# Decoder layer: the cross-attention units of a query tile handled in pairs, their value matmuls placed behind the self-attention values in four column groups of 32

## Chip, cores, metric

One NeuronCore of a Trainium2 chip runs the whole program. The metric is device time in microseconds (us) of one launch, lower is better.

## The reference

Thirty-two independent sequences ("batches") of 256 tokens and 256 features go through one decoder layer, in fp32. Each step adds its input and is followed by a layer norm without weights.

```python
x = layernorm(x + self_attention(x))       # 16 heads of 64, 4 key/value heads, rotary, ALiBi
x = layernorm(x + cross_attention(x, ctx)) # 16 heads of 16, layer norms with weights ahead of all four
                                           # projections; a query sees the keys of its window of 64 and
                                           # of the window before, causal, and only where cell ids agree
x = layernorm(x + feed_forward(x))         # silu(gate) * up -> down, 256 -> 1024 -> 256, weights rounded
                                           # to three values, activations to 8 bits
```

## The kernel before

Tokens are cut into two query tiles of 128 for each batch. Self-attention of a batch is eight units (`self_units`: tile, key/value pair, head pair), two to a **period**. A period is four **slots**, and the loop at the end of the kernel writes out by hand, slot by slot, the order of all work of TensorE (PE), VectorE (DVE) and ScalarE (ACT). A batch has four periods, and batch follows batch without a gap. The other parts of a layer are generators that start at a given slot (`at`) and give one piece of work whenever `parts()` is called: projections (`self_inputs`), `self_output`, `cross_inputs`, `cross_output`, `feed_forward`. So at any time PE serves the self-attention of one batch, the cross attention and feed-forward of the batch before, and the projections of the next. The queue of SyncE (SP) issues nearly all transfers, in the order of the program.

In one period the order of a self unit pair `2m`, `2m+1` is: scores (tile `s`, L393, four matmuls of two 64-row blocks for each unit), reductions on DVE (L409, adding the ALiBi bias and keeping the maximum), exponentials on ACT (L427), transposes on PE (tile `t`, L471), copies out on ACT (L480). In the first slot of the next period come the values (tile `o`, L492, two column blocks of 64), then a normalizing product on DVE (L505), which waits for reciprocals that travel through a DMA transpose (`wide`, `planes`) and a GpSimd copy (`R`). `self_output` (tile `wo`, L513) follows for each query tile.

Cross attention has four units for a batch, one to a period, four periods behind (`CROSS = 4`): a unit is one query tile `qc` and one half `ch` of the 16 heads. Its steps are

- `cross_scores` in slot 1: tile `xs` in four PSUM banks, L674, blocks of 32 rows of the array. Query tile 0 is one span of 128 queries; tile 1 is two spans of 64 queries, each with its own keys, so its blocks are 32 rows by 64 columns. Then eight reductions on DVE (L688, mask added), 128 x 128 each;
- `cross_exp` in slots 2 and 3, on ACT (L704);
- `cross_turn` in slot 0 of the next period: transposes (`xt`, L713) and a copy on ACT (`xpT`, L715);
- `cross_values` in slot 1 of that period: tile `xo`, L729, four column blocks of 32, copied out by ACT (`xoT`, L738);
- `cross_back` in slot 2: transposes (`xr`, L749), reciprocal and product on DVE (L754, L755) into `on`.

`cross_output` (tiles `zoT`, `xw`) and `feed_forward` (`ff` gate and up, L816; `ffo`, L863; tanh on ACT, L830; products on DVE, L831 and L837) follow. PSUM has eight banks in one pool, all tiles of 128 x 512 fp32 share them. Buffers in SBUF have a number of copies, the last argument of `work`.

The order of the slots before:

```python
if part == 0:   # scores and exponentials of the two self units, then
    pair(self_values, m - 1)
    cross(cross_turn, k - 1, 0); cross(cross_turn, k - 1, 1)
elif part == 1:
    parts(); cross(cross_scores, k); cross(cross_values, k - 1)
elif part == 2: # self transposes and copies, then
    cross(cross_exp, k, 0); cross(cross_back, k - 1)
else:           # self transposes and copies, then
    cross(cross_exp, k, 1)
```

Of the kernel before, what the change touches and what calls it, by code (L numbers as in the profile page):

```python
# [9 lines left out]
F32 = mybir.dt.float32  # L10
# [3 lines left out]
AF = mybir.ActivationFunctionType  # L14
# [3 lines left out]
P = 128  # L18
L = 256
NT = L // P  # L20
D = 256
# [30 lines left out]
def kernel(  # L52
# [50 lines left out]
    def work(name, shape, bufs=2, dtype=F32):  # L103
        return sb.tile(list(shape), dtype, tag=name, name=name, bufs=bufs)

    def small(name, n):
        return sb.tile([P, 8], F32, tag="small", name=name, bufs=48)[:, 0:n]
# [100 lines left out]
    def prepare_cross():  # L208
# [4 lines left out]
        for j, (w, dst) in enumerate(  # L213
# [13 lines left out]
            if j == 0:  # L227
                nc.sync.dma_start(wo_sb, Wo.rearrange("(c p) n -> p c n", p=P))
            if j in xbias:
                more = work("xp", [P, 512])  # L230
                row = more[:, 0:D]
                nc.sync.dma_start(row, rows[j].partition_broadcast(P))
                for dc in range(NDC):
                    nc.gpsimd.tensor_scalar(
                        more[:, D + dc * P : D + (dc + 1) * P],
                        ones,
                        vecs_sb[:, j, 1, dc : dc + 1],
                        None,
                        ALU.mult,
                    )  # L240
# [238 lines left out]
        for pT, pt in zip(s["pT", i], s.pop(("t", i))):  # L479
            nc.scalar.copy(pT, pt)  # L480

    def self_values(b, m):

        s = state[b]
        qc, kc, _rp = self_units[2 * m]
        pTs = [s.pop(("pT", 2 * m + rp)) for rp in range(2)]
        s["oT", qc, kc] = oT = work("oT", [P, NCH // 2, P], 3)
        po = bank("o")
        for kk in range(NT):
            for rp in range(2):  # L490
                for half in range(2):
                    nc.tensor.matmul(  # L492
                        po[half * HD : (half + 1) * HD, rp * L : (rp + 1) * L],
                        s["v"][:, kk, (2 * kc + half) * HD : (2 * kc + half + 1) * HD],
                        pTs[rp][half][:, kk * L : (kk + 1) * L],
                        start=(kk == 0 and rp == 0),
                        stop=(kk == NT - 1 and rp == 1),
                    )
        s["po", m] = po

# [6 lines left out]
    def self_output(b, qc):  # L507
# [24 lines left out]
        yield  # L532
        zq = work("row", [P, D], 4)

        s["x1", qc] = x1 = work("x1", [P, D], 3)

        def residual():
            nc.vector.tensor_scalar(zq, h, mv[:, 0:1], rs[:, 1:2], ALU.subtract, ALU.mult)
# [120 lines left out]

    cross_units = [(qc, ch) for qc in range(NT) for ch in range(NDC)]

    spans = {0: ((0, P, 0, 0),), 1: ((0, 64, 64, NT), (64, P, P, 1))}

    def cross_scores(b, i):
        s = state[b]
        qc, ch = cross_units[i]

        banks = [bank("xs") for _ in range(4)]  # L670
        for q0, q1, k0, _t in spans[qc]:
            for r in range(4):
                rows_ = slice(r * 32, (r + 1) * 32)
                nc.tensor.matmul(  # L674
                    banks[r][:, 0 : 2 * P].rearrange("p (h k) -> p h k", k=P)[q0:q1],
                    s["xqT", qc][rows_, ch, q0:q1],
                    kTz[rows_, ch, :, k0 : k0 + P],
                    start=True,
                    stop=True,
                    tile_position=(r * 32, q0),  # L680
                )
        s["xnm", i] = [small("xnm", 4) for half in range(2)]
        for half in range(2):
            s["xp", i, half] = p = work("xp", [P, 512])
            for j in range(XHH):
                cols = slice(j * P, (j + 1) * P)

                nc.vector.tensor_tensor_reduce(  # L688
                    p[:, cols],
                    banks[2 * half + j // 2][:, j % 2 * P : (j % 2 + 1) * P],  # L690
                    s["mask"][:, qc, :],
                    -1.0,
                    3.0e38,
                    ALU.add,
                    ALU.min,
                    s["xnm", i][half][:, j : j + 1],
                )

    def cross_exp(b, i, half):
        s = state[b]  # L700
        p = s["xp", i, half]
        for j in range(XHH):
            cols = slice(j * P, (j + 1) * P)
            nc.scalar.activation(  # L704
                p[:, cols], p[:, cols], AF.Exp, bias=s["xnm", i][half][:, j : j + 1], scale=-1.0
            )

    def cross_turn(b, i, half):
        s = state[b]
        p = s.pop(("xp", i, half))  # L710
        pt = bank("xt")
        for j in range(XHH):
            nc.tensor.transpose(pt[:, j * P : (j + 1) * P], p[:, j * P : (j + 1) * P], ident)  # L713
        s["xpT", i, half] = pT = work("xpT", [P, 512])
        nc.scalar.copy(pT, pt)  # L715

    def cross_values(b, i):


        s = state[b]  # L720
        qc, ch = cross_units[i]
        po = bank("xo")
        for half in range(2):
            pT = s.pop(("xpT", i, half))
            h0 = ch * 2 * XHH + half * XHH
            for q0, q1, _k, t in spans[qc]:
                for j in range(XHH):
                    e0 = (t * XH + h0 + j) * XE
                    nc.tensor.matmul(  # L729
                        po[j * 32 : (j + 1) * 32, half * P + q0 : half * P + q1],  # L730
                        s["xv"][:, e0 : e0 + 32],
                        pT[:, j * P + q0 : j * P + q1],
                        start=True,
                        stop=True,
                        tile_position=(0, j * 32),
                    )
        s["xoT", i] = oT = work("xoT", [P, 2 * P])
        nc.scalar.copy(oT, po[:, 0 : 2 * P])  # L738

    def cross_back(b, i):  # L740

        s = state[b]
        qc, ch = cross_units[i]
        oT = s.pop(("xoT", i))
        if ch == 0:
            s["on", qc] = work("on", [P, D])
        pt = bank("xr")
        for half in range(2):
            nc.tensor.transpose(  # L749
                pt[:, half * P : (half + 1) * P], oT[:, half * P : (half + 1) * P], ident  # L750
            )
        po = pt[:, 0 : 2 * P].rearrange("p (h e) -> p h e", e=32)
        rinv = small("xrinv", 2 * XHH)
        nc.vector.reciprocal(rinv, po[:, :, XHD])  # L754
        nc.vector.tensor_tensor(  # L755
            s["on", qc][:, ch * P : (ch + 1) * P].rearrange("p (h e) -> p h e", e=XHD),
            po[:, :, 0:XHD],
            rinv.unsqueeze(2).to_broadcast([P, 2 * XHH, XHD]),
            ALU.mult,
        )  # L760

# [121 lines left out]
    def at(slot, gen):  # L883
        starts.setdefault(slot, []).append(gen)
# [5 lines left out]
    for b in range(B):  # L890
        s0 = 16 * b
        if b:
            at(s0 - 15, self_inputs(b))
        at(s0 + 2, cross_inputs(b))
        for t in range(NT):
            at(s0 + 9 + 8 * t, self_output(b, t))
            at(s0 + 4 * CROSS + 11 + 8 * t, cross_output(b, t))
        at(s0 + 4 * CROSS + 26, feed_forward(b))

    with tc.manual_schedule(engines={mybir.EngineType.PE, mybir.EngineType.DVE, mybir.EngineType.Activation}):  # L900
        running = []
        slot = min(starts)
        while starts or running:
            m, part = divmod(slot, 4)
            k = m - CROSS
            for gen in starts.pop(slot, ()):
                running.append([slot, gen])

            def cross(f, unit, *more):
                if 0 <= unit < 4 * B:  # L910
                    f(*divmod(unit, 4), *more)

            def pair(f, unit):
                if 0 <= unit < 4 * B:
                    f(*divmod(unit, 4))

            def own(f, unit, *more):
                if 0 <= unit < 8 * B:
# [11 lines left out]
            if part == 0:  # L930
                own(self_scores, 2 * m)
                own(self_exp, 2 * m, 0)
                own(self_exp, 2 * m, 1)
                flush()
                own(self_scores, 2 * m + 1)
                own(self_exp, 2 * m + 1, 0)
                pair(self_values, m - 1)
                cross(cross_turn, k - 1, 0)
                cross(cross_turn, k - 1, 1)
                parts()  # L940
                own(self_exp, 2 * m + 1, 1)
                pair(self_normal, m - 1)
            elif part == 1:
                parts()
                cross(cross_scores, k)
                cross(cross_values, k - 1)
            elif part == 2:
                pair(self_inverse, m)
                parts()
                own(self_turn, 2 * m)  # L950
                own(self_copy, 2 * m)
                cross(cross_exp, k, 0)
                cross(cross_back, k - 1)
            else:
                own(self_turn, 2 * m + 1)
                parts()
                own(self_copy, 2 * m + 1)
                cross(cross_exp, k, 1)
                pair(self_spread, m)
            if part < 3:  # L960
                flush()
# [91 lines left out]
```

## Time and profile before

| | us |
|---|---|
| median of 3 runs (lowest, highest) | 2183.65 (2179.22, 2185.29) |
| profiled execution, its span | 2184.1 |
| PE matmul busy | 2096.9 |
| PE weight loads busy | 1606.7 |
| DVE busy | 1778.0 |
| ACT busy | 1600.0 |
| GpSimd busy | 1285.1 |

The profile is of one execution. It gives the span from the first to the last instruction and no other time of its own, so the span is taken as its time; it lies 0.5 us from the median of the runs. Ends of matmuls are modelled in it, starts are measured. A group is one line, tile and shape; "xcount" counts records, and a matmul of fp32 operands leaves two, a transpose or a bf16 matmul one.

### The profile page before, as it was taken

The page shows a single profiled execution, that of the slowest core. Times are in us where ns is not written, and L with a number is a line of the kernel's source. Part 1 is how long each engine was busy: PE and PEld are TensorE (multiplying, and loading weights), DVE is VectorE, ACT ScalarE, POOL GpSimd, SP SyncE. Part 2 cuts the span into 40 slices and gives each one's busy share as a digit, 9 for nine tenths or more (in the row PEclk, how much of TensorE's full clock was granted, in tenths as well). Part 3 has the DMA queues.
Part 4 walks back from the last instruction along what each step waited for, and adds up shares of the span by engine and source line. Part 5 has one row for each costly group of instructions (what it writes and reads, how often), then busy time and mean ns, then how long its engine had stood idle before and what let it go on. Part 6 is the DMA issues. An engine that isn't in the chain of part 4 may idle for free.

```text
span 2184.1 us, 54367 instructions
## 1 busy us (share of the span) xinstructions
PE 2096.9 (96%) x17316; PEld 1606.7 (74%) x17316; DVE 1778.0 (81%) x6949; ACT 1600.0 (73%) x4833; POOL 1285.1 (59%) x1977
## 2 busy tenths in 40 slices
PE   7899999999999999999999999999999999999983
PEld 5677777777777777777777777777777777777751
DVE  4777888888888888888888888888888888888765
ACT  2478778777778877777877777877777877777862
POOL 4555665566655656655656655656666566666542
PEclk9899999999999999999999999999999999999986
DMA  7432333333333334334334333333343333333211
GB/s 219 111 75 72 82 75 83 77 79 86 89 72 78 83 71 91 86 71 86 76 76 89 82 77 79 78 81 83 86 82 76 81 82 74 90 81 69 53 42 32
DMA packets 326589, 177.57 MB, mean 81 GB/s; under 512 B 242976, under 2 KB 296096, under 8 KB 326304
## 3 DMA queue, kind: packets, MB, share of 16 engines
q1 hardware_dynamic: 324608, 170.52, 34.6%
q8 instruction: 139, 2.28, 0.5%
q10 hardware_dynamic: 1696, 3.57, 0.5%
q14 instruction: 146, 1.20, 0.2%
HBM read 39.50 MB, written 8.39 MB: 22 GB/s over the span
## 4 chain that ended last, share of the span: by engine, by line
PE 74%; DVE 11%; ACT 5%; POOL 4%; DMA 4%; issue 1%; SPq 0%; ACTq 0%; POOLq 0%; DVEq 0%
PE wo L513 10%; PE o L492 8%; PE proj L330 8%; PE t L471 8%; PE s L393 8%; PE ff L816 5%; PE xt L713 4%; PE xo L729 3%; PE xq L550 3%; PE xs L674 3%; PE ffo L863 3%; PE xk L622 3%; DVE p L409 2%; PE xw L775 2%; PE v L362 2%; DVE xib L805 2%
## 5 line engine op out<-in xcount | busy, mean ns | idle before, releaser
L427 ACT ACTIVATE p<-p,nm 128x256 f32<-128x256 f32 x1024 | 511.6, 512 | 197.7 <-DVE nm L409 197.7
L409 DVE CUSTOM_DVE_ANT_0 p<-s,alibi 128x256 f32<-128x256 f32 x1024 | 364.6, 416 | 6.3 <-PE s L393 6.3
L480 ACT COPY pT<-t 128x512 f32<-128x512 f32 x512 | 276.1, 601 | 89.6 <-PE t L471 89.3
L704 ACT ACTIVATE xp<-xp,xnm 128x128 f32<-128x128 f32 x1024 | 331.8, 416 | 0.0
L688 DVE CUSTOM_DVE_ANT_0 xp<-xs,mask 128x128 f32<-128x128 f32 x1024 | 225.9, 285 | 68.1 <-PE xs L674 68.1
L455 POOL COPY R<-planes 128x1024 uint16<-128x1024 uint16 x128 | 175.4, 1370 | 176.3 <-DMA planes<-wide 164.6
L471 PE MATMUL t<-ident,p 128*128 128x128 f32 x2048 | 266.4, 273 | 0.9 <-ACT p L427 0.9
L492 PE MATMUL o<-pT,v 128*64 128x256 f32 x2048 | 260.8, 386 | 1.3 <-ACT pT L480 1.1
L393 PE MATMUL s<-kT,qT 64*128 64x256 f32 x2048 | 255.7, 389 | 0.0
L513 PE MATMUL wo<-wo_sb,oT 128*128 128x256 f32 x1024 | 248.0, 386 | 0.4 <-ACT xpT L715 0.3
L354 POOL TENSOR_TENSOR qT<-qT,other 128x512 f32<-128x512 f32 x128 | 169.4, 1323 | 127.6 <-DMA other<-psin 66.4
L330 PE MATMUL proj<-xT,wq_sb 128*128 128x256 f32 x1024 | 243.1, 381 | 0.0
L471 PEld LDWEIGHTS t<-ident,p 128*128 128x128 f32 x2048 | 234.2, 141 | 9.4 <-ACT p L427 2.6
L393 PEld LDWEIGHTS s<-kT,qT 64*128 64x128 f32 x2048 | 187.3, 186 | 63.4 <-issue 14.3
L492 PEld LDWEIGHTS o<-pT,v 128*64 128x64 f32 x2048 | 143.9, 136 | 104.4 <-issue 21.2
L513 PEld LDWEIGHTS wo<-wo_sb,oT 128*128 128x128 f32 x1024 | 194.9, 193 | 30.9 <-ACT xpT L715 1.1
L427 ACT ACTIVATION_READ_ACCUMULATOR p<-p,nm 128x1 f32 x1024 | 208.0, 203 | 0.0
L330 PEld LDWEIGHTS proj<-xT,wq_sb 128*128 128x128 f32 x1024 | 185.8, 191 | 21.1 <-issue 0.4
L831 DVE SCALAR_TENSOR_TENSOR gu<-gu,ff 128x512 f32<-128x512 f32 x128 | 82.6, 684 | 84.5 <-ACT gu L830 84.3
L713 PEld LDWEIGHTS xt<-ident,xp 128*128 128x128 f32 x1024 | 110.6, 141 | 53.7 <-issue 38.5
L713 PE MATMUL xt<-ident,xp 128*128 128x128 f32 x1024 | 143.3, 281 | 2.1 <-ACT xp L704 2.0
L339 DVE TENSOR_TENSOR psin<-proj,rs_sb 128x512 f32<-128x512 f32 x160 | 109.8, 686 | 38.2 <-PE proj L330 34.6
(146 smaller groups left out, 4325.7 us busy)
## 6 DMA issues: line engine op xcount, KB each, us to landing
other<-psin SPq DMA_DIRECT2D x640, 64.0 KB, 2.0
xT<-in_xt_dram SPq DMA_DIRECT2D x32, 256.0 KB, 2.8
xs<-in_x_dram SPq DMA_DIRECT2D x32, 256.0 KB, 2.8
cs<-in_ctx_dram SPq DMA_DIRECT2D x32, 256.0 KB, 2.8
other<-qb SPq DMA_DIRECT2D x64, 128.0 KB, 2.1
kTz<-tr SPq DMA_DIRECT2D x256, 32.0 KB, 2.0
other<-qb SPq DMA_DIRECT2D x128, 64.0 KB, 2.0
out_dram<-x SPq DMA_DIRECT2D x32, 256.0 KB, 2.3
```

The lines of the kernel that those rows point to most:

```text
L330: nc.tensor.matmul(pq[:, c * L : (c + 1) * L], w[:, dc, c * P : (c + 1) * P], xT[:, dc, :], start=(dc == 0), stop=(dc == NDC - 1),)
L393: nc.tensor.matmul(banks[half][:, rr * L : (rr + 1) * L], qT[rows_, rr, qc * P : (qc + 1) * P], kT[rows_, kc, :], start=(rr == 0), stop=(r ...
L409: nc.vector.tensor_tensor_reduce(p[:, cols], banks[half][:, cols], alibi[:, 2 * (4 * kc + 2 * rp + rr) + half, :], -0.125, 3.0e38, ALU.add ...
L427: nc.scalar.activation(p[:, cols], p[:, cols], AF.Exp, bias=nm[:, rr : rr + 1], scale=-1.0, accum_out=s["sums", i // 2][:, e : e + 1],)
L455: nc.gpsimd.tensor_copy(R.bitcast(U16).rearrange("p (n z) -> p z n", z=2), s.pop(("planes", m)).rearrange("p z r q -> p z (r q)"),)
L471: nc.tensor.transpose(pt[:, j * P : (j + 1) * P], p[half][:, rr * L + kk * P : rr * L + (kk + 1) * P], ident,)
L480: nc.scalar.copy(pT, pt)
L492: nc.tensor.matmul(po[half * HD : (half + 1) * HD, rp * L : (rp + 1) * L], s["v"][:, kk, (2 * kc + half) * HD : (2 * kc + half + 1) * HD], ...
L513: nc.tensor.matmul(py[:, 0:D], s["oT", qc, kc][:, r, :], wo_sb[:, 4 * kc + r, :], start=(kc == 0 and r == 0), stop=(kc == 1 and r == 3),)
L688: nc.vector.tensor_tensor_reduce(p[:, cols], banks[2 * half + j // 2][:, j % 2 * P : (j % 2 + 1) * P], s["mask"][:, qc, :], -1.0, 3.0e38, ...
L704: nc.scalar.activation(p[:, cols], p[:, cols], AF.Exp, bias=s["xnm", i][half][:, j : j + 1], scale=-1.0)
L713: nc.tensor.transpose(pt[:, j * P : (j + 1) * P], p[:, j * P : (j + 1) * P], ident)
```

## The change

Both cross units of a query tile go together, in every second period. In an even period slot 1 computes the scores of both halves of the heads (8 matmuls for tile 0, where a unit had 4, and 16 for tile 1, where a unit had 8) into the same four banks, now full, and DVE makes 16 reductions. The exponentials stay spread, two parts in each period. In an odd period's first slot, `self_values` is cut into four column blocks of 32 (before: two of 64), and the cross values of the tile before stand directly behind it, in the same block shape; `cross_turn` of the first two parts follows, and that of the other two comes an even period later. `cross_back` handles a whole tile, once in two periods. Cross output and feed-forward start four slots (a period) later. `xp` and `xpT` have four copies in place of two, `x1` four in place of three, `xoT` one of double width, and the scratch space of the DMA descriptors is set to 1024 bytes.

```diff
-    def self_values(b, m):
+    def self_values(b, m, w):
...
-                for half in range(2):
+                for g in range(P // w):
+                    e0 = 2 * kc * HD + g * w
                     nc.tensor.matmul(
-                        po[half * HD : (half + 1) * HD, rp * L : (rp + 1) * L],
-                        s["v"][:, kk, (2 * kc + half) * HD : (2 * kc + half + 1) * HD],
-                        pTs[rp][half][:, kk * L : (kk + 1) * L],
+                        po[g * w : (g + 1) * w, rp * L : (rp + 1) * L],
+                        s["v"][:, kk, e0 : e0 + w],
+                        pTs[rp][g * w // HD][:, kk * L : (kk + 1) * L],
...
+                        tile_position=(0, g * w),
...
-    def cross_scores(b, i):
+    def cross_scores(b, qc):
...
         for q0, q1, k0, _t in spans[qc]:
-            for r in range(4):
-                rows_ = slice(r * 32, (r + 1) * 32)
-                nc.tensor.matmul(
-                    banks[r][:, 0 : 2 * P].rearrange("p (h k) -> p h k", k=P)[q0:q1],
+            for ch in range(NDC):
+                for r in range(4):
+                    rows_ = slice(r * 32, (r + 1) * 32)
+                    nc.tensor.matmul(
+                        banks[r][:, ch * 2 * P : (ch + 1) * 2 * P].rearrange("p (h k) -> p h k", k=P)[q0:q1],
...
-    def cross_values(b, i):
+    def cross_values(b, qc):
...
-        for half in range(2):
-            pT = s.pop(("xpT", i, half))
+        for part in range(4):
+            pT = s.pop(("xpT", qc, part))
...
-        s["xoT", i] = oT = work("xoT", [P, 2 * P])
-        nc.scalar.copy(oT, po[:, 0 : 2 * P])
+        s["xoT", qc] = oT = work("xoT", [P, 4 * P], 1)
+        nc.scalar.copy(oT, po)
...
-            at(s0 + 4 * CROSS + 11 + 8 * t, cross_output(b, t))
-        at(s0 + 4 * CROSS + 26, feed_forward(b))
+            at(s0 + 4 * CROSS + 15 + 8 * t, cross_output(b, t))
+        at(s0 + 4 * CROSS + 30, feed_forward(b))
...
-            k = m - CROSS
+            n, odd = divmod(m - CROSS, 2)
...
-                pair(self_values, m - 1)
-                cross(cross_turn, k - 1, 0)
-                cross(cross_turn, k - 1, 1)
+                pair(self_values, m - 1, 32 if odd else HD)
+                if odd:
+                    cross(cross_values, n - 1)
+                    cross(cross_turn, n, 0)
+                    cross(cross_turn, n, 1)
+                else:
+                    cross(cross_turn, n - 1, 2)
+                    cross(cross_turn, n - 1, 3)
...
-                cross(cross_scores, k)
-                cross(cross_values, k - 1)
+                if not odd:
+                    cross(cross_scores, n)
...
-                cross(cross_exp, k, 0)
-                cross(cross_back, k - 1)
+                cross(cross_exp, n, 2 * odd)
+                if odd:
+                    cross(cross_back, n - 1)
...
-                cross(cross_exp, k, 1)
+                cross(cross_exp, n, 2 * odd + 1)
```

## The prediction

> **What bounds the kernel now.** I read the page first: busy shares, then the slices and the chain of waits.
>
> ```profile
> PE 2096.9 (96%) x17316; PEld 1606.7 (74%) x17316; DVE 1778.0 (81%) x6949; ACT 1600.0 (73%) x4833; POOL 1285.1 (59%) x1977
> ...
> PEclk9899999999999999999999999999999999999986
> ...
> PE 74%; DVE 11%; ACT 5%; POOL 4%; DMA 4%; issue 1%; SPq 0%; ACTq 0%; POOLq 0%; DVEq 0%
> ```
>
> PE is busy all the time at full clock, and the chain runs through it. A busy PE can still lose time inside its rows, so next I cut the steady stretch and one batch at the starts of its four periods:
>
> ```profile
> 115.00:2073.00 1958.00, 1937.93 (x16294) 1496.15 (x16292) 1643.63 (x6500) 1505.57 (x4564) 1192.42 (x1830) 1.00 0.36 79
> ```
> ```profile
> 924.47:939.10 14.63, 14.62 (x128) 10.85 (x127) 11.09 (x48) 12.03 (x38) 6.19 (x10) 1.00 0.32 64
> 939.10:953.82 14.72, 14.72 (x119) 11.68 (x118) 14.13 (x58) 12.96 (x41) 7.83 (x12) 1.00 0.28 59
> 953.82:975.33 21.51, 21.51 (x163) 17.39 (x162) 17.45 (x66) 14.47 (x44) 15.40 (x28) 1.00 0.38 84
> 975.33:989.47 14.14, 13.45 (x136) 9.65 (x135) 11.89 (x47) 10.45 (x34) 10.31 (x15) 1.00 0.46 114
> ```
>
> The columns after the length are PE, PEld, DVE, ACT and POOL busy. 1958 us are about 30.3 batches of 64.6 us, and PE has 20 us of holes in them. So a batch lasts as long as PE's groups stand apart. The timeline of PE gives that distance: each group's start against the next start (the second column is modelled and not used).
>
> ```profile
> 1004.10 2.00 PE L393 MATMUL s<-kT,qT 64*128 64x256 f32 x16
> 1006.02 1.95 PE L492 MATMUL o<-pT,v 128*64 128x256 f32 x16
> 1007.90 1.09 PE L713 MATMUL xt<-ident,xp 128*128 128x128 f32 x8
> ...
> 1009.38 1.89 PE L330 MATMUL proj<-xT,wkv_sb 128*128 128x256 f32 x8
> 1011.21 0.71 PE L674 MATMUL xs<-kTz,xqT 32*128 32x256 f32 x8
> 1011.85 0.65 PE L729 MATMUL xo<-xpT,xvaug 128*32 128x128 f32 x16
> 1012.43 1.16 PE L550 MATMUL xq<-zT,xq_w 128*128 128x128 f32 x8
> 1013.42 1.89 PE L362 MATMUL v<-wkv_sb,xT 128*128 128x256 f32 x8
> 1015.15 0.38 PE L204 MATMUL zoT<-ident,on 128*128 128x128 f32 x2
> 1015.37 1.04 PE L471 MATMUL t<-ident,p 128*128 128x128 f32 x8
> 1016.24 0.38 PE L749 MATMUL xr<-ident,xoT 128*128 128x128 f32 x2
> ```
>
> An fp32 matmul is two records. Values v takes 1.73 for 8 records of 256 columns, 0.216 each; a transpose of 128 columns 0.87/8 = 0.109. The same work ahead of xs, proj, takes 1.83. The figure after the names (64*128, 128*64, 32*128, 128*32) is the tile shape of the array. Where it changes, PE loses about 0.1 on leaving and again on entering: s 1.92 for 8 pairs that stream in 1.73, o 1.88 for 1.73, xs 0.64 for two rounds of 0.216, xo 0.58 for four rounds of 0.109. Six such changes stand in every period, twelve per query tile. That is what the change touches.
>
> **Part by part**, per batch of two query tiles, in us of PE:
>
> Scores. Four groups xs (0.64 twice for tile 0, 0.62 twice for tile 1, whose blocks are 32*64) become two, each with two rounds more than one group had: 0.64 + 2 x 0.216 = 1.07 and 0.62 + 0.43 = 1.05. 2.52 becomes 2.12: -0.40. Two of four exits ahead of xs go (1.83 - 1.73): -0.20.
>
> Tile 1 needs care. Its loop emits, for the first half of the queries, both units on four row blocks, then the second half in the other column half. The row for today's order:
>
> ```profile
> 1029.71 0.47 PE L674 MATMUL xs<-kTz,xqT 32*64 32x256 f32 x8
> ```
>
> In a window of 0.06 us, eight of sixteen records start: both halves run side by side although the first half's second passes stand ahead of the second half in program order. In the new order 16 passes stand ahead of it, not eight. If PE still finds it, four rounds remain (1.05). If it is held until the first half has only its last rounds left, there are six to eight, +0.43 to +0.86 per batch. I take the first, as the eight starts at once are the nearest row, and keep the other as a rival. The Trainium skill, "TensorE: Matmul & The Clock Gate", Part 3, "What overlaps and what doesn't", says that matmuls start and end strictly in program order, no reordering. The row above does not agree for the two passes of one call; by the rule the tile would take some seven rounds, 0.65 more per batch, 20 us in all.
>
> Values. Four groups xo (0.58 each, today entering from xs) become two of doubled length behind o of the same 128*32 shape: 8 rounds x 0.109 + 0.10 for leaving = 0.97 (tile 1: twice the rounds at half the columns). 2.34 becomes 1.94: -0.40. The two o ahead of them no longer leave their shape: -0.20. Cutting those o into four blocks of 32 doubles their instructions (16 calls for 8) but not the streaming: four column blocks run at once, as xo shows at 0.109 per four; 8 rounds x 0.216 = 1.73 stays. Returning to the full array costs xq 0.99 - 0.90 = 0.1 today (twice a batch, the bf16 groups behind xo next to nothing); after, wo or xk behind xs pay the same 0.1 twice: 0.
>
> Sum: -0.40 - 0.20 - 0.40 - 0.20 = -1.20 per batch, x 30.3 batches = -36.
>
> Waits that go. Today xo needs xpT of the same period:
>
> ```profile
> 982.55 0.69 PE L674 MATMUL xs<-kTz,xqT 32*64 32x256 f32 x16
> 983.63 0.91 PE L729 MATMUL xo<-xpT,xvaug 128*32 128x64 f32 x32 [0.39 <-ACT xpT L715]
> ```
>
> Over 29 batches the fourth period's xs and xo stand 20 us further apart in sum than their medians. After, xo reads copies made at least one period earlier, so these waits go. But ACT is what was late there (the exp rows of L427 and L704, the copies L480), and gates of the feed-forward move with it, by one period: summing its rows in the new order gives ACT 12.9, 12.1, 12.2, 12.0 for PE periods of about 13.1, 17.0, 18.8, 13.7. The first is 98% full, so the next late thing is pT for o or t's input there. I credit half: -10 (ends: -20 and +25).
>
> DVE. Its 16 reductions (L688, 225.9/1024 = 0.22 each) come at once, 3.5 us every second period instead of 1.8 in each. Behind them in DVE's order stand rinv and wide, the tanh products, row, and the next period's self reductions (L409); PE's t takes the xs banks when reductions 10 to 16 are over (2.2 to 3.5 us after they begin), and has 2.9 us (gates 0.95, zoT 0.22, wo 1.73) or 3.7 us (xk, zoT, wo) of other groups first. That covers the first bank. DVE's sums in the new order are 11.1, 12.6, 17.2, 13.0 for the same periods, at most 95%, no fuller than today's 14.13 of 14.72, which PE got through without a hole. So nothing is added; uncovered, it would cost up to 1.8 per tile. The merged back step saves a reciprocal, the wider xoT copy an access: both off the path. Extra buffers and the smaller descriptor scratch issue nothing; SP's queue has the same DMAs, and kTz's wait for the last scores gets earlier by a period.
>
> Ends. Cross output and feed-forward start one period later. At the start PE is already full by then. At the end one more period stands behind the last self unit; the last periods there are 5 to 10 us apart (xs at 2107.41, 2117.10, 2122.54), while the work that moves into it leaves the full stretch (2 to 3 us), and both units' scores come a period early. I take +3 (ends -3, +10).
>
> Total on the profiled execution: its span of 2184.1 is its own time as far as recorded (0.5 from the median 2183.65), so 2184 - 36 - 10 + 3 = 2141.
>
> **Rivals.**
> (B) The second half of tile 1's scores runs after the first: +0.43 to +0.86 per batch, 13 to 26 us, 2154 to 2167. For it: no group today shows PE passing a block that has four passes waiting. Against: it passes two.
> (C) Slower: the 16 reductions hold banks and the self reductions behind them, and PE waits for t or s in every second period. Fully exposed, 1.77 x 61 = 108 us: 2249. It decides from (36 + 10 - 3)/61 = 0.7 us per tile. Against: 2.9 us of PE work stand between, and by the sums above DVE still idles 2.0 and 1.6 us in the periods that receive them.
> (D) ACT in the first period becomes late for o and t. Today one such wait is 0.38 (o in a first period starts 991.47 and xt 993.73, 2.26 against 1.88); one and a half to three more a batch are 15 to 35 us, 2156 to 2176. For it: the 98%. Against: today's fourth period asks more of ACT, 14.6 by the same sum in 14.1, and loses only 0.7.
> (E) The change does not do what it says: PE still drains between o and xo, because the shapes of their outputs differ. Twice 0.15 a batch comes back: +9, 2150.
>
> **How the numbers follow.** Forecast 0.52, B 0.20, D 0.13, E 0.06, C 0.09. The range 2124 to 2172 takes all waits gone (2184 - 36 - 20 - 3 = 2125) at its low end and B and most of D at its high end; C and part of D are left out. A measurement of this kernel can tell 0.3%, 6.5 us: faster is below 2177, which is A, B, E and nearly all of D, less a reserve for mixtures of them: 0.85; same 0.05; slower 0.10.
>
> **What would show it.** Right: o with 32 columns to xo about 1.78 (no 0.1 at the end), xo 0.97, xs 1.07 (x16) and 1.05 (x32), periods of a batch summing to about 63, no wait of xo for xpT. B: xs x32 at 1.5 to 1.9. C: t or s waiting for DVE L688, L409 in the first and third period. D: o or t waiting for ACT in the first. E: 0.1 more at o's end. I am wrong if a batch still takes 64.6.

## The result, and the profile after

The changed kernel takes 2367.13 us in the median of 4 runs (2360.39 to 2371.95), the kernel before 2184.47 beside it: 1.083 times as long, 95% interval 1.081 to 1.086. The forecast was 2141. The profiled execution has a span of 2368.2.

The engine line of the page after:

```profile
PE 2128.0 (90%) x18278; PEld 1676.8 (71%) x18340; DVE 1743.5 (74%) x6821; ACT 1594.4 (67%) x4769; POOL 1282.5 (54%) x1977
```

PE is idle for a tenth of the span, where it was idle for 4%. No other engine has a larger share of the span than before; all are emptier. So nothing became the new bound by its work: PE waits. Cut at the starts of four periods in a row, the second, third and fourth of one batch and the first of the next (columns as in the prediction, the 1.00 or 0.91 is the granted clock):

```profile
1012.15:1028.96 16.81, 16.76 (x187) 13.74 (x188) 13.09 (x40) 15.43 (x46) 8.43 (x17) 1.00 0.31 70
1028.96:1047.83 18.87, 18.87 (x144) 15.23 (x143) 15.92 (x71) 12.65 (x39) 12.50 (x16) 1.00 0.25 63
1047.83:1066.71 18.88, 15.03 (x147) 12.53 (x146) 13.01 (x38) 8.75 (x28) 11.91 (x19) 0.91 0.55 94
1066.71:1084.85 18.14, 14.97 (x99) 10.76 (x99) 12.29 (x67) 12.87 (x39) 7.55 (x14) 0.91 0.31 73
```

The second and third period are 16.81 and 18.87, without a hole, as summed in the prediction (17.0 and 18.8). The fourth and the first have holes and a lower clock. Over 26 batches the means of periods one to four are 17.5, 16.8, 18.9, 17.7 (sum 70.9); before 14.6, 14.7, 21.6, 13.9 (64.9); forecast 13.1, 17.0, 18.8, 13.7. Two waits carry it, in PE's own list (us in total, times, longest):

```profile
PE xs L674 <- POOL xqT L588: 75.0, 28, 8.1
PE xt L713 <- DVE qT L346: 71.9, 28, 3.8
```

Each comes about once a batch. In the fourth period `xt` needs a PSUM bank that VectorE's `qT` product has to release, and that product stands behind `hib`, which waits for GpSimd. PE, VectorE and GpSimd in one such place:

```profile
1051.51 1.06 PE L727 MATMUL xo<-xpT,xvaug 128*32 128x128 f32 x32
1056.41 1.89 PE L713 MATMUL xt<-ident,xp 128*128 128x128 f32 x8 [3.85 <-DVE qT L346]
```
```profile
1053.30 1.77 DVE L850 TENSOR_SCALAR hib<-gu 128x1024 bf16<-128x1024 f32 x1 [6.42 <-POOL gu L847]
...
1055.59 0.67 DVE L346 TENSOR_TENSOR qT<-proj,rs_sb 128x512 f32<-128x512 f32 x1
```
```profile
1042.49 3.20 POOL L614 TENSOR_SCALAR mask<-ck_i,cq_sb 128x128 f32<-128x128 f32 x3 [0.41 <-DVE xnm L690]
...
1050.53 0.40 POOL L605 CAST ck_i<-ck_i 128x256 f32<-128x256 int32 x1 [1.57 <-DMA ck_i<-in_cell_k_dram]
...
1052.15 1.12 POOL L847 TENSOR_SCALAR gu<-gu,ffhup 128x1024 f32<-128x1024 f32 x1
```

VectorE stands for 6.42 us, though the scaling itself takes 1.12: GpSimd does the mask and the key rotation first, and stands 1.57 for the transfer of the cell ids (`ck_i`). In the first period `xs` waits for `xqT`, the rotated query, also from GpSimd. And after a hole PE runs slowly for some microseconds (the clock is the third figure from the right):

```profile
1073.18:1076.30 3.12, 0.17 (x1) 0.00 (x0) 0.69 (x1) 2.75 (x9) 2.89 (x5) 1.00 0.34 105
1076.30:1078.34 2.04, 2.04 (x16) 1.39 (x17) 0.54 (x5) 0.00 (x0) 0.00 (x0) 0.66 0.00 0
1078.34:1080.41 2.07, 1.85 (x6) 1.05 (x7) 2.07 (x21) 0.83 (x2) 0.00 (x0) 0.51 0.00 0
```

So the 16 records of `xs` take 2.04 where they take 1.08 without a hole.

### The profile page after: what moved, and what is told of

The parts are those of the page before. It is cut to its first block, busy times and chain, and to the rows that moved or that the text cites. A ratio compares the mean times of both kernels' runs of the same rounds, so it can differ in the third digit from the quotient of the medians.

```text
span 2368.2 us, 55762 instructions
## 1 busy us (share of the span) xinstructions
PE 2128.0 (90%) x18278; PEld 1676.8 (71%) x18340; DVE 1743.5 (74%) x6821; ACT 1594.4 (67%) x4769; POOL 1282.5 (54%) x1977
## 5 line engine op out<-in xcount | busy, mean ns | idle before, releaser
L354 POOL TENSOR_TENSOR qT<-qT,other 128x512 f32<-128x512 f32 x128 | 163.8, 1280 | 225.8 <-DMA other<-psin 110.2
L471 PE MATMUL t<-ident,p 128*128 128x128 f32 x2048 | 256.1, 273 | 1.8 <-ACT p L427 0.9
L515 PE MATMUL wo<-wo_sb,oT 128*128 128x256 f32 x1024 | 254.6, 394 | 0.0
L493 PE MATMUL o<-pT,v 128*32 128x256 f32 (+1 forms) x3072 | 252.8, 385 | 1.3 <-ACT pT L480 1.2
L471 PEld LDWEIGHTS t<-ident,p 128*128 128x128 f32 x2048 | 232.8, 141 | 13.2 <-ACT p L427 2.6
L713 PE MATMUL xt<-ident,xp 128*128 128x128 f32 x1024 | 157.9, 298 | 75.1 <-DVE qT L346 71.9
L493 PEld LDWEIGHTS o<-pT,v 128*32 128x32 f32 (+1 forms) x3072 | 133.0, 119 | 103.6 <-issue 19.9
L713 PEld LDWEIGHTS xt<-ident,xp 128*128 128x128 f32 x1024 | 119.6, 150 | 116.4 <-issue 110.9
L850 DVE TENSOR_SCALAR hib<-gu 128x1024 bf16<-128x1024 f32 x64 | 76.5, 1195 | 151.1 <-POOL gu L847 151.1
L455 POOL COPY R<-planes 128x1024 uint16<-128x1024 uint16 x128 | 172.3, 1346 | 10.3 <-DMA planes<-wide 10.3
L674 PE MATMUL xs<-kTz,xqT 32*64 32x256 f32 (+1 forms) x1536 | 93.0, 416 | 85.4 <-POOL xqT L588 75.0
```

Of the source, the lines that this page charges most:

```text
L455: nc.gpsimd.tensor_copy(R.bitcast(U16).rearrange("p (n z) -> p z n", z=2), s.pop(("planes", m)).rearrange("p z r q -> p z (r q)"),)
L471: nc.tensor.transpose(pt[:, j * P : (j + 1) * P], p[half][:, rr * L + kk * P : rr * L + (kk + 1) * P], ident,)
L493: nc.tensor.matmul(po[g * w : (g + 1) * w, rp * L : (rp + 1) * L], s["v"][:, kk, e0 : e0 + w], pTs[rp][g * w // HD][:, kk * L : (kk + 1) * L],
L515: nc.tensor.matmul(py[:, 0:D], s["oT", qc, kc][:, r, :], wo_sb[:, 4 * kc + r, :], start=(kc == 0 and r == 0), stop=(kc == 1 and r == 3),)
```

## Experiments

Ratios are against the kernel before on the same chip (2185 to 2187 in each set), with 95% intervals.

**Is it the shift or the new unit order?** First theory: the four slots by which `cross_output` and `feed_forward` start later bring their steps into collision with others (theory P). Rival: the 16 reductions in a burst. `shift_only` is the kernel before with nothing but

```diff
-            at(s0 + 4 * CROSS + 11 + 8 * t, cross_output(b, t))
-        at(s0 + 4 * CROSS + 26, feed_forward(b))
+            at(s0 + 4 * CROSS + 15 + 8 * t, cross_output(b, t))
+        at(s0 + 4 * CROSS + 30, feed_forward(b))
```

and the fourth copy of `x1` and the scratch size that go with it.

> The kernel before, with one part of the change alone: cross output and feed-forward start one period later (x1 with four copies). Cross units, scores, values and block shapes stay as before. Theory P (GpSimd's order: the moved steps stand behind cross_inputs' mask and key rotation, and ahead of the query rotation): the loss is in this part, and without the gain of 36 from fewer shape changes it is larger than the change itself: 2300 to 2420 us, DVE's hib waiting for GpSimd's gu by over 100 us in sum. Rival R (the burst of 16 cross reductions and the fuller banks): nothing of it is here, so 2175 to 2200 us.

2333.52, ratio 1.068 (1.066 to 1.070). The shift alone costs 147 us, without one edit to the matmuls or the reductions, so the rival is not the cause of these. The time lies in the range of theory P, but by luck: VectorE's `hib` waits 5.4 us for GpSimd in sum, not over 100. The run has one hole, ahead of the first period's `xs`, 4.2 us a batch; its fourth period is 13.6 and clean.

So the fourth period's hole in the changed kernel does not come from the shift alone. With the shift alone GpSimd does the second scaling in the third period, and the mask late in the fourth (which starts at 1106.85), behind that period's reductions:

```profile
1103.44 1.13 POOL L852 TENSOR_SCALAR gu<-gu,ffhup 128x1024 f32<-128x1024 f32 x1 [2.48 <-DVE ffhup L848]
...
1118.55 2.89 POOL L612 TENSOR_SCALAR mask<-ck_i,cq_sb 128x128 f32<-128x128 f32 x3 [1.82 <-DVE xnm L688]
```

In the changed kernel all reductions of query tile 1 are made in the third period. The mask follows right behind them (the 0.41 in the row further up), and so it stands, with the key rotation, ahead of the scaling. What the new order of units adds to the shift can only be estimated: 182 less 147, and the 35 us that the matmul shapes gained (below), make about 70 us. No run has the pairing without the shift, so the part of the reductions' new place is argued from these rows and not shown. Nor has a run the shift without the smaller scratch; the transfers `other<-psin` take 0.58 us to issue and 2.0 to land with either size.

**The first repairs, of the fourth period's hole,** three edits to the changed kernel. `hib_on_dve`: `nc.vector` for `nc.gpsimd` in L847. `mask_early`: the four mask instructions two slots earlier in the program. `ff_two_later`: `feed_forward` at +34.

> The changed kernel, with the feed-forward's scaling ahead of hib (gu times ffhup plus the rounding constant) on DVE in place of GpSimd. Theory P: DVE's wait of 151 us for that step is gone, and with it PE's 72 us ahead of xt and some of the half-clock time: the fourth period falls from 17.8 to about 14.5 and the whole to 2200 to 2280 us; PE's wait of xs for xqT in the first period may stay. Rival R: DVE gets two instructions of about 0.7 us more per batch and gets later, 2370 to 2420 us.

> The changed kernel, with the four GpSimd instructions of the mask (3.4 us) issued two slots earlier, right behind the conversion of the cell ids, so that they leave GpSimd's queue between the two scaling steps of the feed-forward. Theory P: hib waits some 3 us less per batch, 151 falls to about 60 us, the whole to 2250 to 2320 us. Rival R: no change, 2355 to 2380 us.

> The changed kernel, with the feed-forward one more period later; cross output stays. Theory P: the scaling step no longer meets the mask and the key rotation on GpSimd; it now stands in the fourth and first period. The wait of hib falls under 30 us, the whole to 2180 to 2290 us, depending on what it does to the query rotation of tile 0. Rival R: the reductions are where they were, 2350 to 2380 us.

All three missed the range of theory P: 2358.56 (1.079, 1.078 to 1.081), 2364.84 (1.083, 1.080 to 1.085), 2470.70 (1.131, 1.129 to 1.133). With the scaling on VectorE the hole ahead of `xt` is gone and the fourth period falls from 17.7 to 14.9, as expected, but the first grows from 17.5 to 20.0 and takes nearly all of it back.

`mask_early` lies in the rival's range, but it tests neither theory: in its trace GpSimd has the mask in the same place as before the edit, behind `qT` and ahead of the key rotation, and again right behind the reductions (0.41 <-DVE xnm). `manual_schedule` names PE, VectorE and ScalarE only; the order of GpSimd and SP is the framework's, not the program's. The section on the kernel before says otherwise of SP, wrongly: in the SP rows further down, `planes` stands between two `other<-qb` that the program issues one right after the other. `ff_two_later` made periods one to three longer (20.5, 21.1, 20.6) and the fourth shorter (11.6): the feed-forward's last matmuls then wait for `hiT` (80 us in total). That is a new collision, not a test of the old one.

**Second theory: the chain of the query's rotation.** `xq` on PE, `qb` on ScalarE, two transfers `other<-qb` on SP, three steps on GpSimd (`qb`, `other`, `xqT`), `xs`. Medians of 20 batches, in us from the start of the fourth period:

| | `qb` starts | first `other<-qb` issued | rotation starts | `xqT` starts | first period's `xs` |
|---|---|---|---|---|---|
| before | 10.3 | 11.5 | 16.9 | 18.4 | 21.7 |
| shift_only | 11.7 | 15.0 | 21.3 | 23.5 | 24.3 |
| after | 15.7 | 20.5 | 24.8 | 26.4 | 27.2 |

Before, `xqT` (0.74 long) was done 2.6 us ahead of `xs`. The shift makes the chain from `qb` to `xqT` 3.7 us longer, and both queues in it contribute. SP, before and with the shift:

```profile
986.75 0.53 SPq L573 DMA_DIRECT2D other<-qb  x1
987.37 1.26 SPq L448 DMA_TRANSPOSE planes<-wide  x1
988.68 0.58 SPq L573 DMA_DIRECT2D other<-qb  x1
```
```profile
1050.83 2.57 SPq L448 DMA_TRANSPOSE planes<-wide  x1
1053.50 1.17 SPq L573 DMA_DIRECT2D other<-qb  x2
```

GpSimd, before and with the shift:

```profile
990.61 1.34 POOL L455 COPY R<-planes 128x1024 uint16<-128x1024 uint16 x1
991.88 0.74 POOL L584 TENSOR_TENSOR qb<-qb,rx_sb 128x256 f32<-128x256 f32 x1
```
```profile
1055.42 0.93 POOL L803 TENSOR_SCALAR tr<-x,ffup 128x256 f32<-128x256 f32 x2
1056.30 1.34 POOL L455 COPY R<-planes 128x1024 uint16<-128x1024 uint16 x1
1058.55 0.23 POOL L184 TENSOR_SCALAR rstd_zo<-mv_zo 128x1 f32<-128x1 f32 x1 [0.92 <-DVE mv_zo L178]
1058.74 0.72 POOL L584 TENSOR_TENSOR qb<-qb,rx_sb 128x256 f32<-128x256 f32 x1
```

With the shift, GpSimd has the feed-forward's rounding (`tr<-x,ffup`, L803) and cross output's `rstd_zo` ahead of the rotation, and even waits there for VectorE. Neither stood there before.

Three runs moved `xq` one slot earlier (`yield 1` for `yield 2` behind `zqT`), to start the chain sooner; in the last the scaling is on VectorE too. One run kept its time and let ScalarE issue the transfers:

```diff
-            nc.sync.dma_start(other[e : P : 2, :], qb[1 - e : P : 2, :])
+            (nc.scalar if n == P else nc.sync).dma_start(other[e : P : 2, :], qb[1 - e : P : 2, :])
```

> The kernel with only the two generators shifted (2333.5 us) and the query projection xq one slot earlier (the generator yields 1 instead of 2 between zqT and xq). Rotation theory: the loss is the chain xq, qb on ACT, the two transfers other<-qb on SP, the rotation on GpSimd, xs. Against before, the transfers stand 1 us later behind qb, and GpSimd takes the rotation 2 us later after them, so xqT ends at 24 us after the start of the fourth period instead of 19. One slot is 3.4 us: most of the 5.5 us by which the first period is longer comes back, 2190 to 2240 us. GpSimd-order theory: GpSimd reaches the rotation when the steps ahead of it are over (mask, qT, rstd_y, the two rounding steps tr, R), whenever its transfers land: 2310 to 2340.

> The changed kernel with xq one slot earlier, which also lets SP issue other<-qb ahead of planes. Rotation theory: the first period (17.4 us) loses its hole and falls to 13 to 14; the hole of the fourth period (xt behind qT behind hib on DVE, 17.8) stays: 2240 to 2290. If the two holes are one chain whose end only moves: 2350 to 2370.

> The changed kernel with xq one slot earlier and the scaling of the hidden row (L847) on VectorE. If these two chains are all that the change added, PE is full again and the prediction's terms hold: 2140 to 2190, four periods of about 13, 17, 19, 14. If the chain of xq is not what holds period one: 2350 to 2360, as with the scaling alone. In between, 2200 to 2300: a third wait comes into view.

> The changed kernel with the two transfers other<-qb of the query issued by ScalarE instead of SP, right behind qb. In the changed kernel they are issued 4.8 us after qb starts (before 1.2), behind a load of xT, four transfers other<-psin and a transpose planes. Rotation theory, SP part: 3 to 4 us of the first period's 4.3 go, 2260 to 2310; GpSimd-order theory: 2340 to 2370, since GpSimd does the rotation after rstd_zo and R all the same.

2481.13 (1.135, 1.133 to 1.136; first two periods 22.9 and 19.3), 2388.14 (1.093, 1.091 to 1.095), 2377.57 (1.088, 1.086 to 1.090), 2309.30 (1.055, 1.054 to 1.057). Of the four expectations only the last held, in its SP range. The earlier `xq` failed three times. In `after_q_early` the first period does fall by 1.7, but the second grows by 2.1, since `xq` of tile 1 now waits for ScalarE's copy of `zqT` (2.0 us a batch); and SP still issued `other<-qb` 4.2 us behind `qb`. The other queue was worth 58 us: no wait of `xs` is left, the fourth period's hole stays (2.6), and a new one of 1.3 is ahead of the first period's `xt`.

**Both repairs, a control, and the shift with the other queue.** `queue_and_hib` joins the two edits. `queue_hib_mask_dve` also makes the mask on VectorE, in the fourth period. `before_act_queue` and `shift_act_queue` have the queue edit alone.

> The changed kernel with both repairs: the query's transfers other<-qb issued by ScalarE, and the scaling of the hidden row (L847) on VectorE. Two-waits theory: the hole xo to xt of the fourth period (2.9 us a batch, gone with the scaling alone) and wo to xs of the first (2.7, gone with the queue alone) go together; left are o and xt of the first period, which wait for ScalarE (1.6 and 1.2 in the run with the scaling alone), and about 1 us of half clock: a batch of 66 to 67 for 70.95, 2200 to 2260. One-chain theory (whichever wait is removed, the next one ends at the same time): no better than the better of the two, 2300 to 2360.

> As the run with both repairs, and the four mask instructions of GpSimd (3.6 us a batch, between the third and the fourth period, ahead of the key rotation, R and rs_x) on VectorE in the fourth period (about 0.7 us there). GpSimd theory: the waits left in the run with the scaling alone (VectorE's row for rs_x 2.2 us, behind it the self reductions, behind these ScalarE's exponentials and copies, behind these o and xt) come from GpSimd's queue; they shrink: 2140 to 2200. ScalarE theory (the first period asks for more ScalarE time than PE leaves): as without it, 2200 to 2260.

> Control: the kernel before, with only the query's transfers issued by ScalarE. There xqT is ready 2.6 us ahead of xs, so an earlier xqT is worth nothing, and 1.2 us more of ScalarE a tile lie beside PE: 2175 to 2195. If the queue is worth something by itself (SP's in-order issue holds up more than this chain): below 2170.

> The kernel with only the two generators shifted (2333.5 us, one hole: wo to xs of the first period, 4.2 us a batch), with the query's transfers issued by ScalarE. Of the 5.1 us by which xqT is late there, SP's part is 1 to 2.5 us, GpSimd's order the rest. SP and GpSimd add up: 2255 to 2300. GpSimd's order alone decides: 2320 to 2340. If SP's queue was the whole cause: 2180 to 2210.

2306.37 (1.055, 1.054 to 1.057): only 3 us better than the queue alone. The holes `xo` to `xt` and `wo` to `xs` are both gone, and PE waits instead in the first period for `o` (2.8 us a batch) and `xt` (1.7), which need ScalarE. The time lies in the range of the one-chain theory, although both holes went together, as the two-waits theory said: other waits took their place. With the mask off GpSimd too: 2269.99 (1.039, 1.036 to 1.041), outside both ranges; the fourth period is 13.34. The control costs 2223.25 (1.018, 1.016 to 1.019), above its range: the edit is no gift. The two issues hold ScalarE for 1.1 us a tile or more, which is the likely reason; in the changed kernel it gained 58 in spite of that. The shift with the queue edit: 2291.38 (1.049, 1.047 to 1.051), 42 less, in the range given for SP and GpSimd adding up.

**GpSimd alone, and SP alone.** The scaling, the feed-forward's rounding (L798) and the mask on VectorE, transfers left on SP: in the changed kernel, in the kernel before, with the shift alone. Then the first of these with the cross inputs a slot earlier (`at(s0 + 1, cross_inputs(b))`, the mask kept in its slot), which moves most of the eight `kTz` transfers out of the fourth period; and that edit alone.

> The changed kernel with three steps of GpSimd on VectorE (the scaling L847, the rounding of the feed-forward's input L798, the mask, which also moves from the third to the fourth period), transfers on SP as in the change. GpSimd has 6.6 us a batch less, VectorE some 4 more. GpSimd theory: the waits of VectorE for GpSimd (hib, xib 2.35 us, row) go, with them the late exponentials and copies on ScalarE, and the rotation is in time: 2140 to 2200, all four periods near 13, 17, 19, 14. SP theory: other<-qb still stands behind four transfers other<-psin and planes, so the hole wo to xs of 2 to 3 us a batch stays: 2250 to 2310.

> Control: the kernel before with the same three steps on VectorE. No such wait holds PE there, so no gain: 2175 to 2200, a little more if VectorE (95% of its fullest period) cannot take them. If GpSimd already cost the kernel before something: below 2170.

> The kernel with only the two generators shifted (2333.5), with the same three steps on VectorE. GpSimd theory: GpSimd reaches the query's rotation 4 to 5 us earlier (mask 3.6 us and rounding 1 us stood ahead of it), so the hole of 4.2 us goes: 2180 to 2230. SP theory: 2290 to 2330.

> As the run with three steps on VectorE (2331), and the cross inputs (key, values, their transfers) one slot earlier, so that SP issues seven of the eight copies kTz (0.64 us each) in the third period instead of the fourth, where they stood ahead of the query's transfers. In the run with three steps on VectorE SP issued without a pause from the start of the fourth period until other<-qb, 5.4 us behind qb (before: 1.2). SP theory: other<-qb comes 3 to 5 us earlier, xqT at 19 to 21 us after the start of the fourth period instead of 24, the hole wo to xs (4.0 us a batch) goes, ScalarE's lateness stays in part: a batch of 63.5 to 66, 2140 to 2220. GpSimd-order theory: GpSimd still has rstd_y, qT, R and rstd_zo ahead of the rotation, the hole shrinks by a third at most: 2290 to 2330.

> The changed kernel with only the cross inputs one slot earlier. SP is relieved in the fourth period, but psin, planes and qb themselves still wait there for VectorE, which waits for GpSimd at hib. Two queues must both be clear: little moves, 2330 to 2370. SP alone decides: the hole of the first period (2.7 us a batch) goes, 2270 to 2310.

2331.31 (1.066, 1.063 to 1.069), above both ranges; control 2190.19 (1.002, 1.001 to 1.003), as expected; shift 2274.06 (1.039, 1.037 to 1.041), between the two ranges. With GpSimd relieved the shift loses 89 us instead of 147 and its `xs` hole halves (from 4.1 to 2.0, by the distance of `wo` to `xs`). In the changed kernel the fourth period is clean (13.35), but the hole ahead of `xs` is 4.0. There the rows point to SP: it issues with hardly a pause from the start of the fourth period (1036) on, and the query's transfers (1054.33) come 4.8 us into the first period:

```profile
1044.63 3.36 SPq L660 DMA_DIRECT2D kTz<-tr  x5
...
1049.18 3.68 SPq L312 DMA_DIRECT2D other<-psin  x4
...
1054.33 1.17 SPq L575 DMA_DIRECT2D other<-qb  x2
```

Emptying SP by moving the key chain did not help: 2356.34 (1.078, 1.076 to 1.080), and alone 2371.47 (1.083, 1.080 to 1.086). In the first of the two the hole ahead of `xs` shrank from 4.0 to 1.6 and the first period from 20.7 to 17.6, but `xk` now waits in the third (1.8 us) and the fourth is 15.3. Both expectations missed, the second by 1.5 us: "little moves" is what it did.

**The last run: every queue at once.** The changed kernel with the three steps on VectorE, the query's transfers on ScalarE, and cross output's last scaling moved from ScalarE, where the shift puts it right ahead of `qb` and it waits for GpSimd's `rstd_x`, to GpSimd:

```diff
-        last.append(partial(scaled, h, h, rstd))
+        nc.gpsimd.tensor_scalar(h, h, rstd[:, 0:1], rstd[:, 1:2], ALU.mult, ALU.add)
```

> The changed kernel with three steps on VectorE (scaling of the hidden row, rounding of the feed-forward's input, mask), the query's transfers issued by ScalarE, and cross output's last scaling (L198 x<-x,rstd_x, which the change puts right ahead of qb in ScalarE's order) on GpSimd instead of ScalarE. Against the run with two repairs and the mask on VectorE (2270, a batch of 67.4): VectorE no longer waits 2.35 us for GpSimd at xib, ScalarE no longer 1.3 to 3 us for rstd_x. If these are the last of the loss, the holes of the first period (xs to ff 2.0, o to xt 1.6, s to o 1.3) shrink to 1 to 2 us in all: a batch of 63.5 to 65.5, 2140 to 2205. If a further queue takes the place of each: 2240 to 2275.

2213.55, ratio 1.012 (1.010 to 1.014): outside both ranges, 154 of the 182 us back. Its windows, first to fourth period, and PE's `o` in the first:

```profile
996.78:1012.89 16.11, 14.46 (x98) 10.05 (x98) 13.52 (x72) 14.14 (x42) 7.38 (x13) 1.00 0.44 100
1012.89:1029.70 16.81, 16.76 (x187) 13.75 (x187) 12.36 (x38) 14.84 (x45) 8.96 (x19) 1.00 0.28 63
1029.70:1048.58 18.88, 18.88 (x144) 15.25 (x143) 17.61 (x71) 12.75 (x39) 9.63 (x11) 1.00 0.36 85
1048.58:1061.90 13.32, 13.32 (x147) 11.19 (x147) 12.98 (x41) 7.04 (x24) 8.68 (x14) 1.00 0.43 76
```
```profile
1000.65 2.00 PE L493 MATMUL o<-pT,v 128*64 128x256 f32 x12 [0.91 <-ACT pT L480]
```

Three of four periods are what the prediction summed (17.0, 18.8, 13.7). The first is 16.9 in the mean, not 13.1: ScalarE has 14.14 us of work in it, after 7.04 in the fourth. No version was found that beats the kernel before.

## Why the prediction was wrong, step by step

**PE's shapes: right, in kind and nearly in size.** Measured start to start: `xs` 1.08 and 1.076 (forecast 1.07, 1.05), `xo` 0.99 and 1.03 (0.97), `o` in four column blocks to `xo` 1.751 (1.78). Scores went from 2.52 to 2.15 a batch (-0.37 for -0.40), values from 2.34 to 2.02 (-0.32 for -0.40), the two `o` from 1.88 to 1.75 (-0.26 for -0.20), the exits ahead of `xs` as said. The sum is -1.15 for the -1.20, some 35 us of the 36. So E is out (no drain between `o` and `xo`), and B is out: tile 1's two halves ran side by side with sixteen passes ahead of the second. The Trainium skill, "TensorE: Matmul & The Clock Gate", Part 3, "What overlaps and what doesn't", says that matmuls start and end in program order. On this point it disagrees with the runs, and the measurement decides.

**Reductions: right.** The 16 at once are hidden; `t` behind `wo` starts 1.73 to 1.75 after it in the third period and, where no hole stands ahead, in the first. C is out: the time went to the slower side, but not by its mechanism.

**The waits of `xo` for `xpT`: gone, as said.** The 12.0 us of that wait in the kernel before are not in PE's list after. Whether the -10 was the right size cannot be seen beside the rest.

**The ends: mis-sized.** Forecast +3 with +10 as the far end; from the start of the last period with self scores to the end it took 121 us after and 110 before, and the first period starts 0.7 later: +12 in all.

**The step that failed is the move of cross output and feed-forward.** The prediction counted it only as gates that move by one period, in the sums of ScalarE and VectorE, and as +3 at the ends. GpSimd's queue was never walked at all, and SP's was passed over with "the same DMAs". That was true of their number and not of their order. Of what was moved, `rstd_y`, the rounding, `rstd_zo`, `rstd_x`, the scaling of the hidden row and the transfers `xiT` and `hiT` now stand close to the query's rotation, the mask or the key rotation in the queues of GpSimd and SP; `shift_only` shows that the move alone costs 147 us. The term should have been about +5 us a batch, and was 0. The same omission hid the second hole: "nothing is added" by the 16 reductions was worked out for PE and VectorE, and the mask, which GpSimd makes right behind them by the rows above, was not in it. A sum of busy times could not show it: before the change GpSimd is busy for 59% of the span, and SP issues for 35 of the 65 us of a batch (though for 11.8 of the 13.9 of its fourth period). What mattered for the first period was a chain through both with 2.6 us to spare.

**D came true, behind the others.** When the two waits are gone, PE waits in the first period for ScalarE, `o` for `pT` as named. The sums of 12.9 in 13.1 assumed that ScalarE works evenly; in the last run it is busy for 7.04 of the 13.32 of the fourth period and has 14.14 in the first. Why it stands in the fourth was followed only in part: in the runs with GpSimd relieved it waits for `rstd_x` and for VectorE's reductions.

**An amplifier that was not in the sum: the clock.** Without waits a batch of the changed kernel would be 62.2 (16.8, 18.9 and 13.3 as in the last run, and 13.2 for the first period's groups at their undisturbed distances), close to the forecast's 62.6. It is 70.9: the two holes are 5.2 of the 8.7, and the rest is groups that take longer behind them. The clock accounts for most of that rest: in the trace's clock record a batch has 6.0 us at half the clock, 3.0 us of full clock lost. Mean granted clock: 0.983 before, 0.944 after, 0.980 in the last run.

What stays open: how the shift's loss divides between SP and GpSimd. In `shift_only` GpSimd's three steps were worth 59 us and the other queue 42. The same edits cost the kernel before 5 and 36; if they cost as much here, the two parts are 64 and 79, together 143 of the 147. The two were not tried together in that kernel. Open too is how the fourth period's hole divides between the shift and the new order of units.

## What to carry to other kernels

When a change moves a generator by a period, list every instruction that it issues, on every queue, GpSimd's and SP's above all, and write down for each what it now stands ahead of; then look for the chain behind it that crosses most engines and ask what slack it has, not how busy the engines are. If those two queues are ordered by the framework, build the changed kernel and read their new order before believing that "nothing is added". One repaired wait proves little: repair all that the trace names at once, and keep a control with the same repairs in the kernel before.

## What the runs showed of the hardware

- A hole of 3.0 us on PE was followed by 4.1 us at a granted clock of 0.66 and 0.51, then 1.00 again; a hole of 4.05 in `shift_only` by 0.57 and 0.72 over 4.8. In the trace's clock record these are stretches at half the clock. In 26 batches of the changed kernel there are 42, of which 38 last 3.41 us and 4 last 6.83, and all start on one grid of 3.41 us; so a stretch of 3.41 costs up to 1.7 us (an estimate, half of it). Of 46 holes of 2.0 us or more 41 were followed by one, of 6 between 1 and 2 us one (the lengths are rough, since ends of matmuls are modelled). The Trainium skill, "TensorE: Matmul & The Clock Gate", Part 1, puts the step down after an idle window of about 3.4 us that runs freely. The runs agree with the length and the free running of the window, but not with the need of a whole idle one: 35 of the 42 stretches followed a hole shorter than 3.4 us, and the measurement decides.
- The second half of tile 1's scores runs beside the first although sixteen passes stand ahead of it in PE's order: 32 records start in four rounds of eight, and the whole takes 1.076 us.
- A transfer issued by ScalarE held that engine for 0.47 us (the first of a pair) and 0.61 (the second), and up to 2.0; one issued by SP took SP about 0.58, a transposing one 1.26. Eight for `kTz`, twenty for the rotated projections and 21 others in a batch make a queue of one engine that is nowhere in the busy shares. The Trainium skill, "DMA: Bandwidth & Descriptors", "Issuing engines are not separate DMA queues", says that issuing from several engines saves only the sequencer's issue time, usually small beside the transfer. In the runs the issue was 0.58 beside 2.0 to the landing; even so, two issues a tile moved off SP were worth 58 us here, and cost 36 in the kernel before.
